# Third layer's attention loop: program order on four engines instead of one, and work dealt out by VectorE's time

## The chip, the core and the metric

The kernel runs on one core of a Trainium2 chip. A core has TensorE (PE in the profile; its weight loads are PEld), VectorE (DVE), ScalarE (ACT), GpSimd (POOL) and SyncE (SP), each with its own queue of instructions, which it takes in order; they meet through semaphores. The metric is the device time of one execution in microseconds, and the median of several runs counts. The kernel before took 3640.07 us (3 runs, 3638.57 to 3646.86).

## The reference

The program computes four blocks in a row on x of shape (8, 512, 128), all in float32. Each block takes a layer norm of x, runs a sequence mixer and a feed-forward net on it, and adds `s * silu(g)`. Only the last block, "layer 3", is touched by the change. Cut to what matters it is:

```python
xn = layernorm(x)
# mixer s: a state-space recurrence in chunks, 4 heads of 64, state 128
proj = xn @ W_in                       # z, x, B, C, dt, A, trap, angles
theta = cumsum(angles * dt)            # K, Q = rope(B, C + bias, theta)
S = (Q @ K.T) * decay * causal         # E in the kernel
y = S @ (c * x) + ein * (Q @ state) + coef * x
s = (y * silu(z)) @ W_out
# feed-forward g: 16 heads, softmax over the QUERIES of each key, no mask
scores = einsum('bqd,bkd->bkq', q, k) / sqrt(128)
out = einsum('bkq,bkv->bqv', softmax(scores), v)
g = l2norm(l2norm(out @ Wo) @ Wff); g = gelu(g)
x = x + s * silu(g)
```

The softmax is the large part: 8 batches x 16 heads x 512 x 512 scores.

## The kernel before

The block is built by `layer3` (L2025) with the class `Layer3`. The 16 heads of a batch are worked off in *units*: a unit is one group of four heads (`g`, 0 to 3) and one tile of 128 keys (`kc`, 0 to 3), so a batch has U = 16 units and the stage has 128. A unit has two halves:

- `scores` (L1960): four matmuls of 128 keys by 512 queries, each into a PSUM bank of its own ("pu"), each on a quarter of TensorE's rows (L1969). VectorE takes the negated maximum of each (`nm`, L1972), ScalarE the exponential with that bias, which also leaves the sum `sm` (L1973).
- `weigh` (L1940), LAG = 2 units later: VectorE inverts the sums (L1946), GpSimd scales the values (`va`, L1947), TensorE adds the products up over four key tiles in the bank "pf" (L1954), and every fourth unit the result `oT` is copied out.

Between the units other work of the block is fitted in. It is written as generators, which hand back control at every `yield`:

- `begin(b)` (L1705): layer norm of batch b, its transpose `xT`, queries, keys, values, and then `parameters` (L1744): the small quantities of the recurrence with a softplus polynomial on VectorE, the reciprocal root `r` on GpSimd (L1702), the angles and their sines.
- `mixer(b, jt)` (L1851): one chunk of 128 positions, four per batch. z and x from one matmul (L1857), kq on GpSimd (L1866), four rope products and two sums on VectorE (L1871 to L1873), decays E (L1878, L1883, masked on GpSimd at L199), two groups of transposes (L1897) copied to `kqT`, E times their product (L1902, L1903), the state (L1908 to L1914), the outputs y (L1920 to L1929), and y's transpose `yT` (L1935).
- `end(b)` (L1975): the output product with Wo, two norms with a product with Wff between, gelu, the product of the recurrence with W_out (L1994), and the store.

All these use PSUM banks of a third kind, "pa". Before, the eight banks are split 5 (pu), 1 (pf), 2 (pa).

Who runs when is set in two ways. TensorE's order is the program's: `manual_schedule(engines={PE})` at L2030. The orders of VectorE, ScalarE and GpSimd are chosen by the framework's scheduler, which simulates the program; scores and weigh get a high priority there (`AHEAD = 300`). The program itself gives the generators one step per unit: of those running, half go between scores and weigh and the rest after. A mixer starts at unit `at(b, jt)`, at the earliest one before its chunk's units, with the first ones spread by three units. `Kern.evac` (L115) copies a bank out with ScalarE and VectorE in turn.

Of the kernel before, what the change touches and what calls it, by code (L numbers as in the profile page):

```python
# [15 lines left out]
ALU = mybir.AluOpType  # L16
# [1598 lines left out]
def softplus(nc, pool, x):  # L1615

    shape = list(x.shape)
    tl = lambda name: pool.tile(shape, F32, name=name)
    e, z, q, p = tl("sp_e"), tl("sp_z"), tl("sp_q"), tl("sp_p")
    nc.scalar.activation(e, x, AF.Abs)  # L1620
    nc.scalar.activation(e, e, AF.Exp, scale=-1.0)
    yield
    nc.vector.tensor_scalar(z, e, 2.0, None, ALU.add)
    nc.vector.reciprocal(z, z)
    nc.vector.tensor_tensor(z, z, e, ALU.mult)
    nc.vector.tensor_tensor(q, z, z, ALU.mult)
    nc.vector.tensor_scalar(p, q, 1.0 / 17, None, ALU.mult)
    for n in range(15, 1, -2):
        nc.vector.scalar_tensor_tensor(p, p, 1.0 / n, q, ALU.add, ALU.mult)
    nc.vector.scalar_tensor_tensor(p, p, 1.0, z, ALU.add, ALU.mult)  # L1630
    nc.vector.tensor_scalar(x, x, 0.0, None, ALU.max)
    nc.vector.scalar_tensor_tensor(x, p, 2.0, x, ALU.mult, ALU.add)


class Layer3:
# [43 lines left out]
    def layernorm(self, x, xn):  # L1679

        k, nc = self.k, self.k.nc
        s1 = self.sp2.tile([P, JT], F32, name="s1")
        nc.vector.tensor_reduce(s1, x, AX.X, ALU.add)
        nc.vector.tensor_scalar(s1, s1, 1.0 / C, None, ALU.mult)
        nc.vector.tensor_tensor(xn, x, bc(s1, 2, C), ALU.subtract)
        r = self.rms(xn, JT, 1e-5)
        nc.vector.tensor_tensor(xn, xn, bc(r, 2, C), ALU.mult)

    def rms(self, x, n, eps, floor=False):


        nc = self.k.nc
        sq = self.tp.tile([P, n, C], F32, name="sq", bufs=1)
        nc.scalar.activation(sq, x, AF.Square)
        ss = self.sp2.tile([P, n], F32, name="ss")
# [5 lines left out]
        r = self.sp2.tile([P, n], F32, name="rs")  # L1701
        nc.gpsimd.tensor_tensor(r, ss, self.k.minus_half.to_broadcast([P, n]), ALU.pow)  # L1702
        return r

    def begin(self, b):  # L1705
# [3 lines left out]
        bt = slice(b * JT, (b + 1) * JT)  # L1709
        xn = tp.tile([P, JT, C], F32, name="xn3", bufs=1)  # L1710
        self.layernorm(self.x[:, bt, :], xn)
        yield
        xT = tp.tile([P, T + 1], F32, name="xT3")
        nc.gpsimd.memset(xT[:, T:], 0.0)
        k.to_features(xn, xT, nt=JT)
        yield
# [8 lines left out]
        nc.scalar.copy(q["kT"], ps)  # L1725
        ps = k.pa()
# [6 lines left out]
        yield  # L1733
# [3 lines left out]
        k.evac(q["V"], ps)  # L1737
        q["oT"] = tp.tile([P, 4, T], F32, name="oT3", bufs=1)
        q["held"], q["po"] = {}, {}
        yield  # L1740
        q["ready"] = True
        yield from self.parameters(q)

    def parameters(self, q):  # L1744
# [8 lines left out]
        for jt in range(JT):  # L1753
# [9 lines left out]
            if jt % 2:  # L1763
                yield
        r = self.rms(raw.rearrange("p j a n -> p (j a) n"), 2 * JT, 1e-5)
# [4 lines left out]
        nc.vector.tensor_scalar(beta[:, 0], beta[:, 0], 0.5, 0.5, ALU.mult, ALU.add)  # L1770
        nc.vector.tensor_scalar(beta[:, 1], beta[:, 1], -0.5, 0.5, ALU.mult, ALU.add)
# [5 lines left out]
        yield  # L1777
# [10 lines left out]
        yield  # L1788
        yield
# [6 lines left out]
        nc.vector.tensor_scalar(flat(v["ell"]), ps[:, 0, :], -1.0, None, ALU.mult)  # L1796
        nc.vector.tensor_tensor(v["eout"], v["eout"], v["c"], ALU.mult)
        yield
# [4 lines left out]
        for jt in range(JT):  # L1803
# [4 lines left out]
            if jt == 1:  # L1808
                yield
        yield  # L1810
# [3 lines left out]
        nc.vector.tensor_reduce(dot, prod, AX.X, ALU.add)  # L1814
        meet = par[:, :, NPAR + 4 :].rearrange("p j (a h) -> p j a h", a=2)
# [8 lines left out]
        yield  # L1824

# [12 lines left out]
        nc.vector.scalar_tensor_tensor(t, n, -TWO_PI[0], theta, ALU.mult, ALU.add)  # L1838
        for part in TWO_PI[1:]:
# [7 lines left out]
        nc.scalar.activation(n, n, AF.Square)  # L1847
        nc.vector.tensor_scalar(of(cos), n, -2.0, 1.0, ALU.mult, ALU.add)
        q.update(v=v, BC=BC, sin=sin, cos=cos, state=None)

    def mixer(self, b, jt):  # L1851
# [3 lines left out]
        tl = lambda name, *shape: mp.tile([P, *shape], F32, name=name)  # L1855
        ps = k.pa()
# [4 lines left out]
        nc.vector.scalar_tensor_tensor(z, z, 1.0, ps[:, 0:256], ALU.add, ALU.mult)  # L1861
        xv = tl("xv3", HM, HP)
        nc.scalar.copy(xv.rearrange("p h d -> p (h d)"), ps[:, 256:512])
        kq = tl("kq3", 2, HM, C)
        bias = cn["kq"].rearrange("p (a h n) -> p a h n", a=2, h=HM)
        nc.gpsimd.tensor_tensor(kq, bc(q["BC"][:, jt], 2, HM), bias, ALU.add)  # L1866
        sn, cs = (bc(q[n][:, jt], 1, 2) for n in ("sin", "cos"))
        x1, x2 = kq[:, :, :, 0:NA], kq[:, :, :, NA : 2 * NA]
        t = [tl(f"rope{i}", 2, HM, NA) for i in range(4)]
        for i, (a, r) in enumerate(((x1, cs), (x2, sn), (x1, sn), (x2, cs))):  # L1870
            nc.vector.tensor_tensor(t[i], a, r, ALU.mult)  # L1871
        nc.vector.tensor_tensor(x1, t[0], t[1], ALU.subtract)
        nc.vector.tensor_tensor(x2, t[2], t[3], ALU.add)  # L1873
        yield
# [6 lines left out]
        E = tl("E3", HM, P)  # L1881
# [3 lines left out]
        xc = tl("xc3", HM, HP)  # L1885
# [3 lines left out]
        if jt < JT - 1:  # L1889
            xe = tl("xe3", HM, HP)  # L1890
            nc.gpsimd.tensor_tensor(xe, xv, bc(v["eout"][:, jt, :], 2, HP), ALU.mult)
        yield
        kqT = tl("kqT3", 2, HM, C)
        for w in range(2):
# [3 lines left out]
            k.evac(kqT[:, w], ps)  # L1898
            yield
# [16 lines left out]
        yield  # L1916
        py = k.pa((P, 2, HM, HP))
        if state is not None:
            for h in range(HM):
                nc.tensor.matmul(py[:, 1, h, :], kqT[:, 1, h, :], state[:, h, :], start=True, stop=True)  # L1920
        for h in range(HM):
            nc.tensor.matmul(py[:, 0, h, :], E[:, h, :], xc[:, h, :], start=True, stop=True)
        nc.vector.tensor_tensor(y, y, py[:, 0], ALU.add)
        if state is not None:
            inter = tl("inter3", HM, HP)
# [4 lines left out]
        yield  # L1930
# [6 lines left out]
        q["mixed"] = jt  # L1937
        yield

    def weigh(self, b, u):  # L1940
# [3 lines left out]
        E, sm = q["held"].pop(u)  # L1944
        heads = lambda a: a.rearrange("p (i v d) -> p i v d", v=4, d=8)[:, :, g, :]
        nc.vector.reciprocal(sm, sm)  # L1946
        nc.gpsimd.tensor_tensor(heads(va[:, kc, 0:C]), heads(q["V"][:, kc, :]), bc(sm, 2, 8), ALU.mult)  # L1947
# [9 lines left out]
        if kc == JT - 1:  # L1957
            k.evac(q["oT"][:, g, :], q["po"].pop(g))

    def scores(self, b, u):  # L1960

        k, nc, q = self.k, self.k.nc, self.q[b]
        g, kc = divmod(u, JT)
        E, sm, nm = (self.ep.tile([P, 4, n] if n > 1 else [P, 4], F32, name=nm) for n, nm in ((T, "at3"), (1, "sm3"), (1, "nm3")))
        q["held"][u] = E, sm
        pus = [k.psum("pu", (P, T)) for _ in range(4)]
        for n, pu in enumerate(pus):
            r = slice(n * 32, n * 32 + 32)
            nc.tensor.matmul(pu, q["kT"][r, kc * P : (kc + 1) * P], q["qT"][r, g, :], start=True, stop=True)  # L1969
        for n, pu in enumerate(pus):  # L1970
            w = slice(n, n + 1)
            nc.vector.tensor_reduce(nm[:, w], pu, AX.X, ALU.max, negate=True)  # L1972
            nc.scalar.activation(E[:, n, :], pu, AF.Exp, bias=nm[:, w], accum_out=sm[:, w])  # L1973

    def end(self, b):  # L1975
# [11 lines left out]
        yield  # L1987
        while q.get("mixed") != JT - 1:
            yield
        s = tp.tile([P, JT, C], F32, name="s3", bufs=1)  # L1990
        ps = k.pa((P, JT, C))
        for jt in range(JT):
            for w in range(2):
                nc.tensor.matmul(  # L1994
                    ps[:, jt, :], q["yT"][:, w, jt, :], cn["W_out"][:, w * C : (w + 1) * C],
                    start=(w == 0), stop=(w == 1),
                )
        nc.scalar.copy(s, ps)
# [163 lines left out]
```

## Time and profile before

| quantity | value |
|---|---|
| median of 3 runs | 3640.07 us |
| the profiled execution's own time | 3631.03 us |
| its span | 3629.3 us |
| PE / DVE / ACT / POOL busy, whole span | 2764.3 / 2336.2 / 1642.4 / 745.4 us |
| layer 3: first constants loaded, to the end | 2628.4 to 3629 us |
| maxima L1972, mean of one | 683 ns |
| exponentials L1973, mean of one | 688 ns |
| mean granted TensorE clock, span / score loop | 0.835 / 0.86 of full speed |

A row of the groups reads: line, engine, operation, tile written <- tiles read, shapes, count | busy time in us, mean ns of one | idle time of the engine just before these instructions, and what ended most of it. A row of waits reads: who waited for whom: us in total, times, longest us. A row of the table of stretches has the busy time and the number of instructions of each engine, then the clock granted to TensorE, the DMA engines' busy share and their rate.

### The profile page before, as it was taken

Reading aid. Unit: us, or ns where it says so; the run is one execution under the profiler, and the core shown is the slowest. Engines: PE = TensorE matmul, PEld = TensorE weight load, DVE = VectorE, ACT = ScalarE, POOL = GpSimd, SP = SyncE. Lnnn points to the kernel's source line nnn. Section 1 sums busy time; section 2 is a strip of 40 time slices with the busy share of each in tenths; the row PEclk is TensorE's granted clock in tenths of the full one; section 3 lists DMA queues with packets and bytes.
Section 4 is the critical chain, followed back from the end, with each engine's and each line's share of the span. In section 5 each row is a group of like instructions: output and inputs, shape, how many; then the busy total and the mean of one; then the engine's idle time right before and its main releaser. Section 6 shows DMA issues by size and latency. Waiting matters only on the chain.

```text
span 3629.3 us, 44988 instructions
## 1 busy us (share of the span) xinstructions
PE 2764.3 (76%) x16390; PEld 1479.4 (41%) x16390; DVE 2336.2 (64%) x6346; ACT 1642.4 (45%) x3207; POOL 745.4 (21%) x845
## 2 busy tenths in 40 slices
PE   6164656512998898799999999998678877778777
PEld 4143444401444454344444444444334444444444
DVE  7989898998583234334445445445478787777776
ACT  5163545512544455233333333333266666655655
POOL 0004050400125553201101101101112222222121
PEclk8585757555789899799899899899878898878989
DMA  4003030311002222100000000000000000000000
GB/s 120 2 2 72 1 81 1 72 49 34 1 2 47 39 42 29 56 1 1 1 1 1 1 1 1 1 1 1 6 15 1 4 4 4 1 3 4 1 4 7
DMA packets 67519, 64.53 MB, mean 18 GB/s; under 512 B 5344, under 2 KB 59616, under 8 KB 66784
## 3 DMA queue, kind: packets, MB, share of 16 engines
q1 hardware_dynamic: 39264, 42.75, 3.8%
q0 software_dynamic: 19712, 14.69, 3.1%
q10 hardware_dynamic: 8320, 4.19, 0.4%
q8 instruction: 129, 2.11, 0.2%
q14 instruction: 94, 0.77, 0.1%
HBM read 43.80 MB, written 17.83 MB: 17 GB/s over the span
## 4 chain that ended last, share of the span: by engine, by line
PE 35%; DVE 16%; ACT 7%; issue 2%; POOL 2%; DMA 0%; POOLq 0%; ACTq 0%; DVEq 0%; SPq 0%
PE pa L1372 6%; PE pu L1390 6%; DVE nm L1972 4%; ACT at L1973 3%; PE pu L1969 3%; PE pf L1954 2%; DVE mpad L1404 2%; PE pf L1435 2%; PE pa L1486 1%; PE pa L1485 1%; ACT at L1422 1%; PE pa L1878 1%; PE pa L1509 1%; PE pa L1359 1%; PE pa L1515 1%
## 5 line engine op out<-in xcount | busy, mean ns | idle before, releaser
L1973 ACT ACTIVATE at<-pu,nm 128x512 f32<-128x512 f32 x512 | 347.9, 688 | 174.3 <-DVE nm L1972 154.5
L1972 DVE TENSOR_REDUCE nm<-pu 128x1 f32<-128x512 f32 x512 | 327.4, 683 | 75.4 <-PE pu L1969 74.8
L199 POOL TENSOR_SCALAR_AFFINE_SELECT at<-at 128x512 f32<-128x512 f32 x184 | 123.6, 672 | 1000.2 <-ACT at L1422 851.7
L1404 DVE TENSOR_REDUCE mpad<-pu 128x2 f32<-128x256 f32 (+3 forms) x256 | 199.2, 819 | 168.1 <-PE pu L1401 168.1
L1422 ACT ACTIVATE at<-pu 128x1024 f32<-128x1024 f32 (+3 forms) x256 | 171.8, 702 | 283.5 <-PE pu L1390 283.2
L1078 ACT ACTIVATE at<-pu,rsqrt 128x1024 f32<-128x1024 f32 (+3 forms) x256 | 191.1, 793 | 191.0 <-PE pu L1073 161.2
L1372 PE MATMUL pa<-hid,f 128*128 128x512 f32 x512 | 222.7, 593 | 0.0
L1969 PE MATMUL pu<-qT,kT 32*128 32x512 f32 x1024 | 203.1, 731 | 2.4 <-ACT at L1973 2.3
L1390 PE MATMUL pu<-qT,kT 32*128 32x512 f32 (+3 forms) x1024 | 160.6, 514 | 56.4 <-DVE mpad L1404 41.8
L748 PE MATMUL pa<-ident,Y 128*128 128x128 f32 x32 | 7.9, 425 | 211.2 <-DVE Y L739 211.2
L1954 PE MATMUL pf<-at,va 128*32 128x512 f32 x1024 | 163.1, 715 | 0.4 <-POOL va L1947 0.4
L1390 PE MATMUL pu<-kT,qT 32*128 32x128 f32 (+3 forms) x1024 | 150.8, 565 | 14.7 <-ACT at L1422 10.5
L548 POOL DMA_INDIRECT xg<-xn_d,idx x48 | 55.1, 1147 | 499.5 <-PE pf L552 318.5
L1372 PEld LDWEIGHTS pa<-hid,f 128*128 128x128 f32 x512 | 96.6, 190 | 119.5 <-issue 118.9
L1493 DVE SCALAR_TENSOR_TENSOR X<-X,u 128x512 f32<-128x512 f32 x56 | 38.7, 691 | 156.7 <-ACT u L1488 156.7
L1073 PE MATMUL pu<-qT,kT 32*128 32x512 f32 (+3 forms) x1024 | 130.3, 513 | 4.9 <-ACT at L1078 3.9
L1016 POOL DMA_INDIRECT f_d<-ys,idx x64 | 105.0, 1640 | 140.0 <-DMA f_d<-ys,idx 85.2
L1947 POOL TENSOR_TENSOR va<-V,sm 128x32 f32<-128x32 f32 x128 | 36.7, 286 | 463.6 <-DVE sm L1946 384.0
L1390 PEld LDWEIGHTS pu<-qT,kT 32*128 32x128 f32 x1024 | 67.3, 196 | 154.4 <-DVE mpad L1404 114.3
L1373 ACT ACTIVATE hid<-pa,f 128x512 f32<-128x512 f32 x64 | 44.0, 688 | 172.5 <-PE pa L1372 172.5
L1083 DVE TENSOR_TENSOR at<-at,ceiling 128x512 f32<-128x512 f32 x72 | 50.0, 695 | 102.3 <-ACT at L1078 91.4
L700 DVE TENSOR_TENSOR Z<-Hs,KE 128x96 f32<-128x96 f32 x510 | 108.8, 253 | 0.9
(610 smaller groups left out, 6682.8 us busy)
## 6 DMA issues: line engine op xcount, KB each, us to landing
w<-in_w_dram SPq DMA_DIRECT2D x24, 512.0 KB, 3.7
f_d<-zeros ACTq DMA_DIRECT2D x8, 512.0 KB
xn_d<-xn SPq DMA_DIRECT2D x8, 512.0 KB, 5.0
w<-in_w_dram SPq DMA_DIRECT2D x16, 256.0 KB, 3.2
w<-in_w_dram SPq DMA_DIRECT2D x24, 128.0 KB
f<-in_f_dram SPq DMA_DIRECT2D x1, 2888.0 KB, 11.9
xn<-in_x_dram SPq DMA_DIRECT2D x4, 512.0 KB, 9.0
Gt<-in_x_dram SPq DMA_DIRECT2D x4, 512.0 KB
```

What stands on the lines that cost most here:

```text
L199: self.nc.gpsimd.affine_select(a, a if src is None else src, pattern, ALU.is_ge, 0.0, base=0, channel_multiplier=-1)
L700: nc.vector.tensor_tensor(z[:, 0:3, v, :], bc(prev[:, v, :], 1, 3), bc(KE[:, o + t, 0:3, :], 2, 4), ALU.mult)
L1073: nc.tensor.matmul(pu[:, n, 0:m], q["kT"][r, g // 2, kc * P : kc * P + P], q["qT"][r, g, kc * P :], start=True, stop=True,)
L1078: nc.scalar.activation(at_[:, i : i + 2, 0:m], pu[:, :, 0:m], AF.Square, bias=k.rsqrt2, scale=32.0**-0.5)
L1372: nc.tensor.matmul(ps, fn[n][:, c0 : c0 + P], src[:, i, :], start=(i == 0), stop=(i == 3))
L1390: self.k.nc.tensor.matmul(pu[:, n, 0:m], a[r, c0 : c0 + P], b[r, q0 : q0 + m], start=True, stop=stop)
L1404: nc.vector.tensor_reduce(top[:, i : i + 2, 16], pu[:, :, 0:m], AX.X, ALU.max)
L1422: nc.scalar.activation(at_[:, i : i + 2, 0:m], pu[:, :, 0:m], AF.Exp, scale=8.0**-0.5)
L1954: nc.tensor.matmul(po[i * 32 : i * 32 + 32, :], va[:, kc, c0 : c0 + 32], E[:, i, :], start=(kc == 0), stop=(kc == JT - 1))
L1969: nc.tensor.matmul(pu, q["kT"][r, kc * P : (kc + 1) * P], q["qT"][r, g, :], start=True, stop=True)
L1972: nc.vector.tensor_reduce(nm[:, w], pu, AX.X, ALU.max, negate=True)
L1973: nc.scalar.activation(E[:, n, :], pu, AF.Exp, bias=nm[:, w], accum_out=sm[:, w])
```

## The change

Four things change in layer 3, and the arithmetic stays.

1. The program's order becomes the order of TensorE, VectorE, ScalarE and GpSimd.
2. Each generator's `yield` now gives an estimate of VectorE's time (us) in the step just done. A function `fill` is called twice per unit, between the second and third exponential and after weigh. It moves every mixer one step, and ends and the oldest begin only while a credit of 1.75 us per fill lasts. `yield 0.0` stands for a step without VectorE work; several stand alone between a step that makes something and the one whose products read it.
3. The PSUM banks are split 4 (pu), 1 (pf), 3 (pa). Copies that alternated between two engines get a fixed one, mostly ScalarE; the mixer's z and x are copied out of PSUM together (`zx`), and z's gate then reads that copy. Several mixer tiles have one buffer instead of two.
4. The reciprocal of the sums and the scaling of the values (`scale`) come out of weigh and run one unit after their scores. `rms` is parted into `squares` and `root`. W_out's product moves from `end` to the last mixer of a batch. In the outputs, E's products stand ahead of the state's. If a batch's parameters aren't finished when its first mixer is due, the rest of them is run out at once.

```diff
+    def squares(self, x, n, of):
+        sq = self.tp.tile([P, n, C], F32, name="sq" + of, bufs=1)
+        self.k.nc.scalar.activation(sq, x, AF.Square)
+        return sq
+    def root(self, sq, n, eps, of, floor=False):
...
+    def turned(self, src, dst, copy):
+        ps = k.pa((P, JT, P))
+        for i in range(JT):
+            k.nc.tensor.transpose(ps[:, i, :], src[:, i, :], k.ident)
+        copy(dst, ps.rearrange("p a b -> p (a b)"))
...
         nc.scalar.activation(z, ps[:, 0:256], AF.Tanh, scale=0.5)
-        nc.vector.scalar_tensor_tensor(z, z, 1.0, ps[:, 0:256], ALU.add, ALU.mult)
-        xv = tl("xv3", HM, HP)
-        nc.scalar.copy(xv.rearrange("p h d -> p (h d)"), ps[:, 256:512])
-        kq = tl("kq3", 2, HM, C)
+        zx = tl("zx3", 512)
+        nc.scalar.copy(zx, ps)
+        xv = zx[:, 256:].rearrange("p (h d) -> p h d", d=HP)
+        kq = one("kq3", 2, HM, C)
...
         nc.gpsimd.tensor_tensor(kq, bc(q["BC"][:, jt], 2, HM), bias, ALU.add)
+        yield 0.0
+        nc.vector.scalar_tensor_tensor(z, z, 1.0, zx[:, 0:256], ALU.add, ALU.mult)
...
         for i, (a, r) in enumerate(((x1, cs), (x2, sn), (x1, sn), (x2, cs))):
             nc.vector.tensor_tensor(t[i], a, r, ALU.mult)
+        yield 1.9
         nc.vector.tensor_tensor(x1, t[0], t[1], ALU.subtract)
         nc.vector.tensor_tensor(x2, t[2], t[3], ALU.add)
-        yield
+        yield 0.8
...
-            k.evac(kqT[:, w], ps)
-            yield
+            (nc.vector.tensor_copy if w else nc.scalar.copy)(kqT[:, w], ps)
+            yield 0.7 * w
+        yield 0.0
...
+    def scores(self, b, u):
...
+        for n, pu in enumerate(pus):
+            nc.vector.tensor_reduce(nm[:, n : n + 1], pu, AX.X, ALU.max, negate=True)
+        for n, pu in enumerate(pus):
+            w = slice(n, n + 1)
+            nc.scalar.activation(E[:, n, :], pu, AF.Exp, bias=nm[:, w], accum_out=sm[:, w])
+            if n == 1:
+                yield
+
+    def scale(self, b, u):
...
+        nc.vector.reciprocal(sm, sm)
+        nc.gpsimd.tensor_tensor(heads(va[:, kc, 0:C]), heads(q["V"][:, kc, :]), bc(sm, 2, 8), ALU.mult)
...
-            k.evac(q["oT"][:, g, :], q["po"].pop(g))
+            nc.scalar.copy(q["oT"][:, g, :], q["po"].pop(g))
...
-        ctx.enter_context(k.banks("l3p", pu=5, pf=1, pa=2))
+        ctx.enter_context(k.banks("l3p", pu=4, pf=1, pa=3))
         L = Layer3(k, ctx, x, A, at, k.out)
-        ctx.enter_context(k.tc.manual_schedule(engines={mybir.EngineType.PE}))
+        E = mybir.EngineType
+        ctx.enter_context(k.tc.manual_schedule(engines={E.PE, E.DVE, E.Activation, E.Pool}))
         U = 4 * JT
-        AHEAD = 300
+        SHARE = 1.75
-        EARLY, EVERY = 10, 3
-        at = lambda b, jt: max(b * U + jt * JT - 1, EARLY + EVERY * (b * JT + jt))
...
+        EARLY, EVERY = 9, 3
+        at = lambda b, jt: max(b * U + jt * JT - 2, EARLY + EVERY * (b * JT + jt))
...
+        def fill():
+            nonlocal credit
+            credit = min(credit, SHARE) + SHARE
+            for works in (mixers, ends, begins):
+                for w in works[:1] if works is begins else list(works):
+                    if works is mixers or credit > 0.0:
+                        cost = next(w, None)
+                        if cost is None:
+                            works.remove(w)
+                        else:
+                            credit -= cost
...
+                    if n == at(b, jt):
+                        for w in begins if "cos" not in L.q[b] else ():
+                            for _ in w:
+                                pass
+                            begins.remove(w)
+                            break
+                        mixers.append(L.mixer(b, jt))
...
+            scores = L.scores(*divmod(n, U)) if n < B * U else iter(())
+            next(scores, None)
+            fill()
+            next(scores, None)
             if LAG <= n < B * U + LAG:
-                with k.tc.high_priority(offset=AHEAD):
-                    L.weigh(*divmod(n - LAG, U))
-            step(len(todo))
+                L.weigh(*divmod(n - LAG, U))
+            if 1 <= n <= B * U:
+                L.scale(*divmod(n - 1, U))
+            fill()
```

## The prediction

> **What bounds the kernel now.** I read the table of stretches first, to size the stage. Only the third layer (numbered 3, the last) is edited; its score loop runs from 2646 to 3602 us.
>
> ```profile
> core 0: us, PE busy (x) PEld busy (x) DVE busy (x) ACT busy (x) POOL busy (x), PEclk, DMA share, GB/s
> 2628.00:2646.00 18.00, 8.59 (x31) 5.57 (x30) 10.83 (x24) 3.46 (x6) 3.56 (x6) 0.72 0.28 105
> 2646.00:3602.00 956.00, 757.09 (x4384) 404.90 (x4386) 727.08 (x1661) 589.00 (x1534) 214.34 (x314) 0.86 0.01 3
> 3602.00:3629.00 27.00, 12.17 (x94) 9.84 (x86) 8.24 (x16) 7.61 (x14) 2.27 (x3) 0.76 0.04 11
> ```
>
> In 956 us no engine is full: VectorE 727 (76%), TensorE 757 (79%), ScalarE 589 (62%). The loop has 128 units of four score tiles. The same table for the maxima's line alone gives the pace: 60 and 64 maxima per 128 us, so 16 units (a batch) take some 128 us, 8 us each, in the middle of the stage.
>
> ```profile
> 2832.00:2960.00 128.00, 38.57 (x60) 0.87 0.01 3
> 3088.00:3216.00 128.00, 40.38 (x64) 0.84 0.01 3
> ```
>
> The waits say who holds whom up: first VectorE's, then TensorE's list over this stretch.
>
> ```profile
> DVE nm L1972 <- PE pu L1969: 74.8, 69, 3.9
> DVE sm L1946 <- ACT at L1973: 47.0, 56, 1.6
> DVE z L1861 <- ACT z L1860: 37.0, 20, 4.4
> ```
>
> ```profile
> PE pa L1857 <- DVE E L1903: 28.8, 8, 5.6
> PE pa L1736 <- DVE E L1903: 19.6, 4, 4.9
> PE pa L1878 <- DVE E L1903: 17.7, 8, 4.2
> PE pa L1935 <- DVE y L1929: 12.8, 7, 3.4
> ```
>
> It is a ring: TensorE stands in its written order behind E or y, which VectorE was given late; the next scores then come late, and VectorE waits for them (74.8 us). Another 84 us it spends on a reciprocal or a gate put down before ScalarE has its input. So the stage is bound by order, and its floor is the fullest engine.
>
> **The floor of each engine after the change.** The costs, from the groups by shape and one unit's timeline:
>
> ```profile
> L1972 DVE TENSOR_REDUCE nm<-pu 128x1 f32<-128x512 f32 x512 | 327.4, 683 | 75.4 <-PE pu L1969 74.8
> L122 DVE COPY kqT<-pa 128x512 f32<-128x512 f32 x35 | 23.8, 681 | 3.8 <-PE pa L1897 3.8
> L120 ACT COPY kqT<-pa 128x512 f32<-128x512 f32 x29 | 17.3, 596 | 14.7 <-PE pa L1897 14.5
> L1863 ACT COPY xv<-pa 128x256 f32<-128x256 f32 x32 | 12.0, 374 | 10.1 <-DVE z L1861 10.0
> L2000 DVE TENSOR_TENSOR zo<-zo,rs 128x512 f32<-128x512 f32 x7 | 13.8, 1977 | 4.1 <-POOL rs L1702 4.1
> ```
>
> ```profile
> 2755.88 1.07 PE L1954 MATMUL pf<-at,va 128*32 128x512 f32 x8
> 2755.98 2.48 DVE L1972 TENSOR_REDUCE nm<-pu 128x1 f32<-128x512 f32 x4 [1.17 <-PE pu L1969]
> ...
> 2756.88 1.16 PE L1902 MATMUL pa<-kqT 128*128 128x128 f32 x8
> ```
>
> VectorE: the built orders show 28 fewer evacuations (15 of oT, 3 each of kqT, zT and xT, 4 of V), each 0.68 us: -19 us. Nothing else leaves or joins it: 727 - 19 = 708 us. ScalarE gets those 28 at 0.59 (+16.5), copies 512 columns instead of 256 in every mixer (32 x (0.59 - 0.37) = +7), and loses 4 table loads at 1.28 (-5): 607 us. GpSimd and the DMA queues issue what they did; the eight output DMAs keep their order.
>
> TensorE's instructions are the same, 757 us by the row. Here the Trainium skill ("Perfetto Trace Analysis", Identifying the Most-Contended Engine) says that matmul busy time does not measure headroom, and to take weight-load time, 405 us here. By the row TensorE would be the floor, 757; by the page it has room. I take neither, but the tightest groups of the trace: scores 1.14 and sums 1.07 per unit (x128 = 283); per mixer transposes 1.32, decays 1.16, z 1.12, products 1.16, outputs 1.06 + 1.10, state 1.00, y 0.44 (8.4, x32 = 267); about 21 per batch for projections and ends (x8 = 168). That is an estimate of 718 us, level with VectorE's 708. So the floor is about 710 to 720, if the order lets them overlap.
>
> **What the new order does to each wait.** The reciprocal moves to the following unit, between two fills, behind at least four more maxima: the 47 us go. z moves a half unit behind its tanh, with zx copied out: the 37 us go too, and the three pa banks are freed by copies on ScalarE. E, the state and y stand on VectorE in the half unit in which TensorE makes their products, never later, and TensorE uses them a unit on: of the waits on E and y nothing should be left.
>
> What is new is that VectorE cannot step past a product which isn't there. Queued behind it are the next four maxima, behind them the exponentials, behind those the next scores. Count from R, the first maximum of a unit. The maxima take 2.48; exponentials begin at R + 0.8 and end at R + 3.5 (4 x 0.67). With four banks the next unit's fourth score needs the last of them, so TensorE is free for other work at R + 3.5 + 1.1 = R + 4.6. If a unit lasts D, that is 4.6 - D after the next R, where VectorE reaches its first product at 2.48 + 0.18 = 2.7.
> - Output products (one unit in four): z 1.12, sums 1.07, outputs 2.1: ready at 8.9 - D, a stall of 6.2 - D.
> - Second transposes: 0.66, sums 1.07, 0.66: ready at 7.0 - D, a stall of 4.3 - D.
> - E: 1.07 + 1.16: ready at 6.8 - D, a stall of 4.1 - D.
>
> I added VectorE's instructions of one middle batch, unit by unit in the built order, at their rows' means: between 3.8 and 11.4, mostly 5 to 7 us. Against these D only two of twelve products stall, 1.4 and 0.5: some 2 us per batch. Two more places: the parameters' last part is run out in one go ahead of the next batch's first mixer, and its cosine waits for ScalarE's two sines and a square (0.63 + 0.61 + 0.62, and a table load of 1.28 if that isn't early): about 3 us with the maxima standing behind. The gelu sits between the second and third exponential, with a load each way (2 x 1.28 + 1.26): it holds exponentials back 3.8 us, which I put at 3 on the path. The fills' other products (Wo alone is 3.7 on TensorE) push scores now and then: between 0 and 8, I take 6, since the two floors are so close. Sum 14 us per batch; over seven (first and last have less of each), 98 us.
>
> z now reads zx from SBUF. The skill ("SBUF — State Buffer", SBUF: two separate sides) speaks against that: a VectorE operation with two SBUF inputs and a GpSimd operation that reads SBUF exclude each other for the whole instruction. The trace agrees for zo above, 1977 ns in the mean against 693 at the least. Read so, each z could wait out kq, a 2.0 us GpSimd row: 32 x 2.0 = 64 us. I take 0: the four rope products behind z wait for that same kq anyway. If kq is late, z only waits in their place.
>
> Ahead of the loop 2 us of parameter matmuls (2644.6 to 2646.6) move behind the first scores, and the ending chain (27 us) keeps its steps; I count both at nothing.
>
> **The sum.** Loop: 708 + 98 = 806 us instead of 956, a gain of 150. The profiled execution took 3631 (span 3629.3): 3481. The median of the runs is 9 above it: 3490. VectorE would be at 88% of the loop.
>
> **The rivals.**
> 1. *The gain stops halfway.* The four banks close a loop over ScalarE: whatever a fill puts between exponentials 2 and 3 (z and zx 1.0, kqT 0.6, tables) delays two scores of the next unit, and the two nearly level floors don't interleave. At 7.0 us a unit the loop takes 896 and the kernel 3580. For it: ScalarE goes to 607 us, and it would need only 1.3 us of stall per unit over 708/128 = 5.5. Against: the D above absorb up to 2 us.
> 2. *Almost no stalls*, 30 us in all: loop 738, kernel 3422. Against: TensorE's estimated 718 beside it.
> 3. *Slower.* Each product of E, kqT and y is met too early in every unit, since ordered VectorE has no other work to put there, where the planner had. It decides from (956 - 708)/128 = 1.9 us of stall per unit. At 2.3 us the loop takes 1002, the kernel 3686. For it: the waits of 3.4 to 5.6 us in TensorE's list, turned round. Against: without any cover D falls to 4.2, 3.6 and 3.3 ahead of the three products, and the stalls come to 2.0 + 0.7 + 0.8 = 3.5 us per four units, where 7.6 are needed.
>
> That the change doesn't take hold is excluded by the built orders: maxima now stand four together throughout, with one reciprocal half a unit later.
>
> **How the numbers follow.** First case 0.60 (own range 3450 to 3550: 58 to 158 us of stall), rival 1 0.20, rival 2 0.08, rival 3 0.12. About 0.2%, 7 us, is what these runs can tell from no change; only the seam of rivals 1 and 3 lies there, 0.02. Faster 0.87, slower 0.11. The range runs to rival 2 below and past the centre of rival 1 above: 3425 to 3600.
>
> **What would show it.** Loop near 806 us, VectorE near 708 of it, over 85%; maxima of a middle batch (64) in about 108 us; no sm or z wait of note on VectorE; TensorE's waits on E and y gone and replaced by short waits on exponentials; VectorE's remaining waits on TensorE at kqT, y and the maxima, under 100 us. Wrong if those waits sum to over 240, if the maxima wait for scores as now, or if the granted clock falls below 0.86: at 0.70, seen in one 50 us stretch, TensorE's 718 would be 882.

## The result, and the profile after

The changed kernel took 3621.46 us (median of 5 runs, 3617.50 to 3629.25); the kernel before, run beside it, 3638.57 (3636.30 to 3646.86). The ratio is 0.9952, with a 95% interval of 0.9937 to 0.9968: 17 us faster, where 150 were forecast, and above the range of 3425 to 3600. The profiled execution lies 8 us above that median (3629.25, span 3627.5), the one of before 8 below its own (3631.03, span 3629.3), so the two traces show how the waits moved, and of the 17 us only 2.

The table of stretches of the changed kernel, over the score loop:

```profile
core 0: us, PE busy (x) PEld busy (x) DVE busy (x) ACT busy (x) POOL busy (x), PEclk, DMA share, GB/s
2646.00:3602.00 956.00, 824.75 (x4424) 437.96 (x4422) 721.85 (x1649) 592.67 (x1563) 202.13 (x315) 0.84 0.01 3
```

The loop still fills the same 956 us, and VectorE is at 76% of it as before (721.85 against 727.08). TensorE is busy 68 us longer (757.09 before), with the same matmuls. Of VectorE's waits in this stretch these matter:

```profile
DVE nm L1988 <- PE pu L1986: 93.2, 49, 6.8
DVE par L1777 <- ACT raw L1776: 30.5, 18, 3.4
DVE E L1925 <- PE pa L1924: 26.7, 19, 4.3
DVE kqT L1919 <- PE pa L1918: 15.0, 10, 3.3
DVE cos L1864 <- ACT turns L1862: 14.9, 8, 1.9
DVE y L1946 <- PE pa L1945: 6.1, 3, 2.5
DVE z L1886 <- ACT zx L1880: 5.3, 8, 2.1
```

The waits that the change was to take away are nearly gone: `sm` fell from 47.0 to 1.1, `z` from 37.0 to 5.3. Others stand in their place, and the sum over all of VectorE's rows is what it was: 224.7 us before, 225.5 after. TensorE's list was turned over as well. Its matmuls no longer wait for E or y (a weight load still does, 3.8 us for y in all); it waits for exponentials (first its matmuls, then its weight loads; the two overlap in time and are not to be added):

```profile
PE pu L1986 <- ACT at L1991: 86.8, 33, 8.9
PEld pu L1986 <- ACT at L1991: 161.1, 151, 9.1
```

The groups by shape show the same from the side of the work, first the scores before, then the changed kernel:

```profile
L1969 PE MATMUL pu<-qT,kT 32*128 32x512 f32 x1024 | 203.1, 731 | 2.4 <-ACT at L1973 2.3
...
L1991 ACT ACTIVATE at<-pu,nm 128x512 f32<-128x512 f32 x512 | 348.0, 690 | 197.3 <-DVE nm L1988 193.8 <-POOL E L199 1.5 <-POOL xc L1907 1.3
L1988 DVE TENSOR_REDUCE nm<-pu 128x1 f32<-128x512 f32 x512 | 318.6, 680 | 93.3 <-PE pu L1986 93.2
L1986 PE MATMUL pu<-qT,kT 32*128 32x512 f32 x1024 | 284.8, 735 | 87.3 <-ACT at L1991 86.8
...
L1886 DVE SCALAR_TENSOR_TENSOR z<-z,zx 128x256 f32<-128x256 f32 x32 | 26.3, 822 | 5.3 <-ACT zx L1880 5.3
```

Read the first three rows of the changed kernel as a circle: exponentials wait for maxima, maxima for scores, scores for exponentials. And look at the scores' busy time. It was 203.1 us before, with 2.4 us of idle time ahead of it and a mean of 731 ns for one; now it is 284.8 with a mean of 735. The single matmul is no slower. A unit's four scores sit on four row groups, and released together they overlap: the timeline shows units of 1.14 us. Now each bank is let go by an exponential of its own, so they often start one after another; a unit's scores keep TensorE busy for 2.2 us in the mean (284.8 / 128), where it was 1.6 (203.1 / 128). One such place, TensorE's timeline:

```profile
3198.80 2.74 PE L1986 MATMUL pu<-qT,kT 32*128 32x512 f32 x4 [3.28 <-ACT at L1991]
3201.47 1.94 PE L2016 MATMUL pf<-at,va 128*32 128x512 f32 x8
...
3203.81 1.92 PE L1899 MATMUL pa<-upto,adt 128*128 128x128 f32 x8
```

After 3.28 us of waiting, the last two scores take 2.74 us, and then the sums and decays, 1.06 each at their tightest, take 1.94 and 1.92. The clock granted in the same place (the third value from the right):

```profile
3195.00:3198.80 3.80, 0.52 (x5) 0.01 (x1) 2.05 (x8) 3.73 (x8) 0.24 (x1) 1.00 0.00 0
3198.80:3201.50 2.70, 2.70 (x8) 0.82 (x10) 2.70 (x8) 1.20 (x3) 0.00 (x0) 0.55 0.00 0
3201.50:3206.00 4.50, 4.50 (x21) 2.74 (x21) 3.85 (x8) 2.81 (x10) 0.24 (x1) 0.51 0.02 4
3206.00:3210.00 4.00, 4.00 (x31) 1.99 (x30) 2.42 (x5) 2.59 (x10) 2.36 (x4) 1.00 0.23 66
```

For 7 us behind the gap TensorE has half of its clock: here it has waited itself slow. (The Trainium skill, "TensorE: Matmul & The Clock Gate", HAM oscillation, puts such a loss of clock behind idle gaps of more than about 3.4 us; the one here is 3.28 in the matmuls and 4.11 in the weight loads.)

By batches, counted from 1 and from first maximum to first maximum: batches 4 to 7 of the eight took 125.7 us each in the mean before and now take 119.4, 119.5, 119.5 and 119.5, where the forecast had 108. Batch 3 takes 147.9 (125.2 before); two of its units take 23.3 and 21.6 us, in which parameters are run out at once. So in the two traces batch 3 alone gives back 23 of the 25 us that batches 4 to 7 gain.

### The profile page after: what moved, and what is told of

The parts are those of the page before. It is cut to its first block, busy times and chain, and to the rows that moved or that the text cites. A ratio compares the mean times of both kernels' runs of the same rounds, so it can differ in the third digit from the quotient of the medians.

```text
span 3627.5 us, 45015 instructions
## 1 busy us (share of the span) xinstructions
PE 2834.9 (78%) x16390; PEld 1512.1 (42%) x16390; DVE 2323.2 (64%) x6318; ACT 1643.5 (45%) x3231; POOL 733.2 (20%) x845
## 4 chain that ended last, share of the span: by engine, by line
PE 41%; DVE 15%; ACT 7%; POOL 2%; issue 2%; DMA 1%; POOLq 0%; ACTq 0%; another core or an unknown queue 0%; DVEq 0%; SPq 0%
PE pa L1372 6%; PE pu L1390 6%; PE pu L1986 5%; PE pf L2016 2%; DVE nm L1988 2%; DVE mpad L1404 2%; ACT at L1991 2%; PE pf L1435 2%; PE pa L1486 1%; PE pa L1485 1%; ACT at L1422 1%; PE pu L1073 1%; PE pa L1509 1%; PE pa L1007 1%; PE pa L1359 1%
## 5 line engine op out<-in xcount | busy, mean ns | idle before, releaser
L1988 DVE TENSOR_REDUCE nm<-pu 128x1 f32<-128x512 f32 x512 | 318.6, 680 | 93.3 <-PE pu L1986 93.2
L1986 PE MATMUL pu<-qT,kT 32*128 32x512 f32 x1024 | 284.8, 735 | 87.3 <-ACT at L1991 86.8
L1986 PEld LDWEIGHTS pu<-qT,kT 32*128 32x128 f32 x1024 | 94.6, 213 | 176.7 <-ACT at L1991 161.1
L1390 PE MATMUL pu<-kT,qT 32*128 32x128 f32 (+3 forms) x1024 | 153.2, 575 | 14.9 <-ACT at L1422 10.7
L1372 PEld LDWEIGHTS pa<-hid,f 128*128 128x128 f32 x512 | 96.6, 190 | 119.5 <-issue 118.9
L1390 PEld LDWEIGHTS pu<-qT,kT 32*128 32x128 f32 x1024 | 67.8, 199 | 155.3 <-DVE mpad L1404 114.8
```

Source lines behind the costliest of these rows:

```text
L1372: nc.tensor.matmul(ps, fn[n][:, c0 : c0 + P], src[:, i, :], start=(i == 0), stop=(i == 3))
L1390: self.k.nc.tensor.matmul(pu[:, n, 0:m], a[r, c0 : c0 + P], b[r, q0 : q0 + m], start=True, stop=stop)
L1988: nc.vector.tensor_reduce(nm[:, n : n + 1], pu, AX.X, ALU.max, negate=True)
```

## The experiments

Each ratio is to the kernel before, run beside it. Where two runs are compared, the difference is that of their ratios, times 3638 us, if nothing else is said.

### Whose order costs

The first theory was that VectorE in program order stands in line behind products. The list of engines in program order was cut down in three ways, and the kernel before was put into its own program order on all four.

```diff
-        ctx.enter_context(k.tc.manual_schedule(engines={E.PE, E.DVE, E.Activation, E.Pool}))
+        ctx.enter_context(k.tc.manual_schedule(engines={E.PE}))                     # only TensorE
+        ctx.enter_context(k.tc.manual_schedule(engines={E.PE, E.DVE}))              # TensorE and VectorE
+        ctx.enter_context(k.tc.manual_schedule(engines={E.PE, E.Activation, E.Pool}))  # all but VectorE
```

Only TensorE:

> The changed program with only TensorE in program order; the scheduler orders VectorE, ScalarE and GpSimd again, without the priority that the kernel before gave to the scores. Theory A (TensorE standing in its scores with four banks eats the gain of the order): the order still gives something, so this is slower than the changed kernel's 3621 us, about 3660. Theory B (units of unlike size under a fixed order eat it): a scheduler can even them out, so this is as fast or faster, 3560 to 3620.

Measured: 3595.12, ratio 0.9877 (0.9839 to 0.9914), 27 us under the changed kernel. The scheduler's orders of this program are better than the program's own.

TensorE and VectorE:

> The changed kernel with program order on TensorE and VectorE alone; ScalarE and GpSimd are ordered by the scheduler. If VectorE's order is what costs against the scheduler's (0.988): as the changed kernel, 0.995. If it is ScalarE's (exponentials behind copies, par behind gelu): as with the scheduler, 0.988.

Measured: 3627.49, 0.9982 (0.9973 to 0.9992), 11 us slower than the changed kernel.

All but VectorE:

> TensorE, ScalarE and GpSimd in program order, VectorE alone ordered by the scheduler. With only TensorE in program order the time was 3595 (0.988 of before), with all four 3621. If VectorE's fixed order is what costs (theory 2): 3590 to 3605. If ScalarE's and GpSimd's cost it: 3615 to 3630.

Measured: 3617.53, 0.9940 (0.9922 to 0.9958). So neither VectorE's order alone nor that of ScalarE and GpSimd alone costs the 27 us: to free VectorE gains 4 us, which the intervals don't tell from nothing, to free the other two loses 11, and only both together gain. That one fixed order is enough to hold the others in step is a reading of this, not shown.

Only TensorE, with scores, weigh and scale at the high priority that they had before:

> The changed program with only TensorE in program order, and scores, sums and scaling in the scheduler's high priority as in the kernel before. If the priority was what evened out the kernel before: better than without it, 0.980 to 0.986. If it only puts VectorE's maxima ahead of what TensorE stands and waits for, as before: 0.990 to 1.000.

Measured: 3606.59, 0.9932 (0.9913 to 0.9951). VectorE's wait for the sums is 76.3 us (57.5 without the priority), and nothing is gained: by the ratios it is 20 us slower than without.

The kernel before, with all four engines in its program order:

```diff
-        ctx.enter_context(k.tc.manual_schedule(engines={mybir.EngineType.PE}))
+        ctx.enter_context(k.tc.manual_schedule(engines={E.PE, E.DVE, E.Activation, E.Pool}))
```

> The kernel before with its program order on all four engines, nothing else changed: its steps have no empty places between a product and its reader. If the order alone is what helps, 3600 to 3630. If the order needs the empty steps and the reciprocal a unit later, which is what I expect, the products are met too early and it is slower than the 3639 of before: 3680 to 3800.

Measured: 4195.22, 1.1540 (1.1494 to 1.1586). The order alone costs 557 us, far more than was expected. The rest of the change (empty steps, moved operations, banks, fixed copies) wins that back, and 17 us more; which part of it does was not taken apart.

### Whose work bounds

Half of the sums of weigh left out (TensorE's work, some 68 us at 1.07 per unit):

```diff
-        for i in range(4):
+        for i in range(4) if kc in (0, JT - 1) else ():
```

> The changed kernel without the products of scores and values for the second and third key tile of each group, so half of these sums is left out: 64 x 1.07 = 68 us less of TensorE, nothing else. If TensorE sets the pace throughout: -68 us, 3553. If VectorE does: 3621. Theory B (each unit lasts as long as its fuller engine): about half, 3585. Theory A (TensorE idles in the scores, so the time isn't its own work): 3600 to 3621.

Measured: 3623.10, 0.9961 (0.9951 to 0.9971): nothing gained. The stretch and one group of this run:

```profile
2646.00:3602.00 956.00, 813.16 (x3936) 470.15 (x3936) 716.99 (x1645) 591.91 (x1563) 202.36 (x316) 0.80 0.01 3
```

With some 480 matmuls fewer TensorE is busy nearly as long, at a granted clock of 0.80 instead of 0.84. Scores went from 285 to 323 us (735 to 792 ns for one) and the products in the third kind of bank from 467 to 490. So 68 us less of TensorE's work gain nothing. Whether its work is no bound, or the lower clock gave the time back, this run alone does not tell.

The maxima taken over half of the columns (VectorE, 134 us of work less, 318.6 to 184.5; the maximum is then that of half the scores):

```diff
-            nc.vector.tensor_reduce(nm[:, n : n + 1], pu, AX.X, ALU.max, negate=True)
+            nc.vector.tensor_reduce(nm[:, n : n + 1], pu[:, 0 : T // 2], AX.X, ALU.max, negate=True)
```

> The changed kernel with each maximum taken over the first 256 of 512 columns, the other half of the columns left out of it: 512 x about 0.27 = 138 us less of VectorE, and the first exponential of a unit starts 0.27 us sooner, the last 1.1 us. If VectorE sets the pace throughout: -138 us, 3483. If TensorE's own work does: 3621. Theory B: about half, 3550. Theory A: the ring from maximum to exponential to next score gets 1.1 us shorter in units where TensorE stands, also some 3520 to 3560; the two theories part in the run with half the sums.

Measured: 3569.28, 0.9808 (0.9771 to 0.9844): 52 us of 134. Of what VectorE is spared on the very link of the circle, more than half is lost again in waits (the maxima's for scores rises from 93 to 110). The edit shortens the circle too, so it does not say how much of the 52 us is VectorE's work as such.

Gelu and the sines replaced by tanh, so that ScalarE loads one table where it loaded 32 (31 loads of 1.28 us less, 40 us in all):

```diff
-        nc.scalar.activation(f, f, AF.Gelu)
+        nc.scalar.activation(f, f, AF.Tanh)
-        nc.scalar.activation(of(sin), t, AF.Sin)
-        nc.scalar.activation(n, t, AF.Sin, scale=0.5)
+        nc.scalar.activation(of(sin), t, AF.Tanh)
+        nc.scalar.activation(n, t, AF.Tanh, scale=0.5)
```

> The changed kernel with tanh in place of the third layer's gelu and sines, so another function is computed there and ScalarE never changes its table in this layer. Each batch loses up to four loads of 1.28 us, 8 x 5.1 = 41 us of ScalarE. Theory C (ScalarE's tables between the exponentials stall the scores; the prediction put 3 us per batch on the path for gelu and part of 3 for the cosine): 20 to 40 us less, 0.984 to 0.990 of before. Theory D (all engines are coupled in one ring, so a wait that is taken away comes back elsewhere): under 10 us, 0.993 to 0.996.

Measured: 3578.84, 0.9854 (0.9835 to 0.9872), some 36 us faster (27 to 44 by the two intervals). ScalarE is 62% busy, and yet most of these 40 us are on the path: a load stands between two exponentials, and the circle runs through them.

The product with Wo, 3.79 us in one piece in the trace, dealt out over several fills (one empty step after each of its four groups):

```diff
+            yield 0.0
```

> The changed kernel with the product with Wo (3.7 us on TensorE in one step) dealt out over five fills, a quarter in each of the first four. Theory B (TensorE's lumps, which the credit in VectorE's time does not count, make VectorE wait 4.25 us for scores there in each batch): 15 to 30 us less, 0.987 to 0.991 of before. Theory D: 0.993 to 0.997.

Measured: 3612.48, 0.9943 (0.9926 to 0.9961), not to be told from the changed kernel's 0.9952. The maxima's wait fell from 93 to 62.5, and the time did not follow.

### Loosening the order

Two scores, other work, two scores:

```diff
-        for n, pu in enumerate(pus):
+        for two in ((0, 1), (2, 3)):
+            for n in two:
...
+            if two == (0, 1):
+                yield
```

> The changed kernel with a unit's four scores parted: two scores with their maxima and exponentials, the first fill, then the other two. Theory A (TensorE stands in the scores, 158 us of waits on exponentials up to 3570 us, while products of the fill stand behind them): it now has the fill's products to do while the third and fourth exponential of the unit before run, so the waits fall below 100 us and the kernel to 3540 to 3590. Theory B (unlike units): no change to speak of, 3610 to 3630. Against both: VectorE meets the fill's products sooner, which alone would make it slower, 3640 to 3700.

Measured: 3695.27, 1.0181 (1.0157 to 1.0206), 83 us slower than the changed kernel.

The first fill after the fourth exponential instead of the second:

```diff
-            if n == 1:
+            if n == 3:
```

> The changed kernel with the first fill behind the fourth exponential instead of between the second and the third. Theory C (what ScalarE does between the exponentials, z and zx 1.0, kqT 0.6, gelu with two table loads 3.8 us, holds back two scores of the next unit): some 12 us per batch come off the scores' wait, 3560 to 3600. Otherwise 3610 to 3630.

Measured: 3639.38, 1.0021 (1.0011 to 1.0030), 25 us slower. The maxima's wait falls to 70, that of the parameters rises to 43. Worked out over the 128 units of its trace, the fourth exponential ends 3.64 us behind its unit's first maximum in the mean (4.67 in the changed kernel), and batches 4 to 7 still take 119.5 us each. So ScalarE's other work between the exponentials is not by itself what holds them.

The credit per fill 2.25 instead of 1.75:

```diff
-        SHARE = 1.75
+        SHARE = 2.25
```

> The changed kernel with 2.25 instead of 1.75 us of credit per fill, so that the parameters of a batch are through, or nearly, when its first mixer is due, and no long stretch of VectorE work is run out at once. Theory B (units of 18.8, 23.3 and 21.6 us in batches 1 and 2, 13.2 us in each later one): these units shrink, and 30 to 60 us come off, 3560 to 3590. If the work has only moved to other units that were full too: 3610 to 3630.

Measured: 3634.87, 1.0012 (1.0000 to 1.0025), 22 us slower. The longest units shrink from 23.3 to 18.4 us, batch 3 stays at 147.2, and batches 5 to 7 grow to 122.9. The maxima's wait is 72.5, but that of y 35.7 instead of 6.1.

Five score banks and two others:

```diff
-        ctx.enter_context(k.banks("l3p", pu=4, pf=1, pa=3))
+        ctx.enter_context(k.banks("l3p", pu=5, pf=1, pa=2))
```

> The changed kernel with the banks of before, five for scores and two for the rest. If the lost fifth score bank is what makes TensorE wait (one score of the next unit could go ahead without an exponential): 3590 to 3610. If the third bank for the rest is worth more, because copies run a half unit later: slower, 3640 to 3700.

Measured: 3636.95, 1.0016 (1.0003 to 1.0028), 23 us slower. Weight loads wait 87.5 us for exponentials instead of 161, the maxima 114.7 instead of 93. In all four runs one wait shrank and another grew. None of these runs isolates the circle itself, since none gives it a second unit of banks.

### Opening the circle

The banks are used up (4, 1 and 3 of eight), so the circle can only be opened with smaller scores. In the next kernels scores are made for 256 of the 512 queries, two heads to a bank from the same row group; maxima and exponentials read those columns twice, so that VectorE and ScalarE do what they did, and a tight unit on TensorE takes 1.14 us as before. The other half of the queries is left out, and two of four heads repeat the scores of their neighbours. A unit then takes two banks: with four, two units fit (ring2), with two, one (ring1).

```diff
-        pus = [k.psum("pu", (P, T)) for _ in range(4)]
+        pairs = [k.psum("pu", (P, 2, T // 2)) for _ in range(2)]
+        pus = [pair[:, i, :] for pair in pairs for i in range(2)]
...
-            r = slice(n * 32, n * 32 + 32)
+            r = slice(n // 2 * 64, n // 2 * 64 + 32)
...
-        ctx.enter_context(k.banks("l3p", pu=4, pf=1, pa=3))
+        ctx.enter_context(k.banks("l3p", pu=2, pf=1, pa=3))   # ring1 alone
```

> The same half of the scores in two banks only, so that the banks hold one unit as in the changed kernel. Both theories: within 25 us of the changed kernel's 3621, since the work of each engine and the depth of the ring are what they are there; the maxima's wait for scores at 75 to 115 us.

Measured: 3678.00, 1.0104 (1.0087 to 1.0121). Its waits are the changed kernel's, somewhat larger; it was expected within 25 us of 3621 and came 55 above. One difference shows in the traces: a unit's first exponential starts 1.39 us behind its first maximum (median of 128 units), in the changed kernel 0.78. So this circle is some 0.6 us longer, and ring1 is no equal of the changed kernel. Why is not shown. Ring2 has the same 1.39, so these two can be compared.

> Scores are made for 256 of the 512 queries, two heads to a bank, each head pair from one row group (so TensorE's time for a unit stays about what it was), and maxima and exponentials read the 256 columns twice, so that VectorE and ScalarE do as much as before; the result for the other half of the queries, and for two of four heads, is left out. A unit of scores takes two banks, the four banks hold two units. If the ring of one unit holds the loop (theory): the exponentials of the unit before are no longer waited for, TensorE's waits of scores for exponentials fall from 248 us (87 of a matmul's, 161 of a weight load's) under 80, the maxima's wait for scores from 93 us under 40, and the run is 50 us or more faster than ring1: 3560 or less. If the fixed order and the products behind it hold it (rival): the waits move to the parameters, the products and the exponentials, and the run is within 15 us of ring1.

Measured: 3591.71, 0.9865 (0.9848 to 0.9882): 86 us faster than ring1, with the same work, and 32 us faster than the changed kernel. TensorE's and VectorE's leading waits in ring1:

```profile
PEld pu L1989 <- ACT at L1994: 157.7, 70, 8.9
PE pu L1989 <- ACT at L1994: 127.2, 62, 8.7
DVE nm L1991 <- PE pu L1989: 105.0, 65, 6.0
```

and in ring2:

```profile
PEld pf L2021 <- POOL va L2008: 97.5, 53, 7.1
DVE nm L1991 <- PE pu L1989: 71.2, 27, 6.6
PE pf L2021 <- POOL va L2008: 65.5, 42, 6.7
```

Scores no longer wait for exponentials (4.4 us of idle time ahead of them, 129.6 in ring1), and their busy time goes from 257.7 us to 173.2. The granted clock of the loop is 0.82, against 0.79 in ring1, which may be a part of the gain. But the maxima still wait 71 us, expected were under 40, and the time missed the expected 3560: in program order TensorE now stands before the sums, for GpSimd's scaled values.

Is that the next bound? Each unit weighed one unit later, with one more buffer of exponentials:

```diff
+LAG3 = 3
...
-        self.ep = self.pool("e", LAG + 2)
+        self.ep = self.pool("e", LAG3 + 2)
...
```

> The kernel with two units of half scores in four banks (3592), with each unit weighed three units after its scores and not two (one more buffer for the exponentials). The same parts of the result are left out as there. If TensorE's waits for GpSimd's scaled values (163 us of the loop) are what took the place of the ring: they fall under 30, and the time to 3535 to 3570. If they only stood in time that VectorE's work needs anyhow: within 12 us of 3592.

Measured: 3615.53, 0.9925 (0.9904 to 0.9945), 22 us slower than ring2. (The 163 us expected away are the two rows above added up, though they overlap.) TensorE's waits for the scaled values are gone (7.5 us are left); TensorE waits for the copies of oT (75.4 us) and the exponentials for maxima 212 instead of 193. So the waits for scaled values had stood in time that was lost anyhow. What is left with the circle open is the order:

> The kernel with two units of half scores in four banks, and only TensorE in the order of the program. If the ring and the fixed order of the other three engines cost in different places, their gains add: 30 less than 3592 or more, 3540 to 3565. If the scheduler's order had its gain from working round the ring: 3580 to 3600.

Measured: 3494.76, 0.9605 (0.9579 to 0.9632). With two units of banks and only TensorE in program order the time comes near the 3490 forecast, but in a kernel that makes half of the scores. Its leading waits on ScalarE and VectorE:

```profile
ACT at L1994 <- DVE nm L1991: 57.7, 49, 4.1
DVE nm L1991 <- PE pu L1989: 34.0, 35, 2.9
```

The exponentials' wait for maxima was 194 in the changed kernel. The two causes do more together than apart: against the changed kernel free orders alone gained 27 us, the open ring alone 32, and both 126. How much the ring alone costs under free orders has no control here (ring1 was not run so).

At last the whole computation, nothing left out: two scores, other work, two scores, as in the split that cost 83 us, but with only TensorE in program order.

> The whole computation: two scores, other work, two scores, with only TensorE in the order of the program. With all four engines in program order this split cost (3695 against 3621), since every two maxima then had a place of their own in VectorE's order. If the scheduler makes use of the looser ring, two banks free while the other two are read: 3530 to 3585, under the 3595 of the unsplit one. If the split only doubles the number of times that scores wait for exponentials: 3600 to 3660.

Measured: 3562.78, 0.9812 (0.9796 to 0.9828). It beats the kernel before by 68 us and the changed one by 51, and the unsplit one with free orders by 24. The same split is a loss under four fixed orders and a gain under one. Why it gains is not shown: weight loads of scores wait as long for exponentials as in the unsplit kernel (79 and 81 us), so that two banks are refilled while the other two are read remains the expectation's reading.

## Why the prediction was wrong

The direction was right, the size was not: 17 us of 150. Step by step:

- *What bounds the kernel, "the stage is bound by order"*: right, and it went on being so. With half of the sums the time stayed (0.9961, at a lower clock), and half of the maxima's columns gained 52 of 134 us.
- *The floors.* VectorE: 708 forecast, 722 measured in the stretch. The step "I take 0" for z reading zx from SBUF was wrong by 13 us: nine of z's 32 instances ran beside a `kq` of GpSimd and took 1.69 to 2.05 us, each ending 0.28 us behind it; the other 23 took 0.42. This agrees with the rule of the Trainium skill ("SBUF — State Buffer", SBUF: two separate sides), which had announced up to 64 us; the collisions all lie in the first three batches. The rest of the 14 is a sum of rows that moved both ways: 8 us came in from ahead of the loop and behind it, the rope products fell by 5 (56.6 to 51.2), zo fell from 13.8 to 5.0, the gelu's input f rose from 6.8 to 12.7. ScalarE: 607 forecast, 593 measured. TensorE's 718: its records show 825, but the scores make 82 us more of that than before, since they were let go one by one. Where the banks and the orders were free, TensorE's records showed 704, VectorE's 702, and the kernel took 3495. So no run contradicts the floors. The Trainium skill's reading ("Perfetto Trace Analysis", Identifying the Most-Contended Engine) that matmul busy time is no good measure of headroom holds here: it rose by 68 us while no work was added.
- *The removed waits*: right. sm (47) fell to 1.1 and z (37) to 5.3 on VectorE, and TensorE's matmuls wait for E and y no more.
- ***The step that failed* is the sum of new stalls, "14 us per batch; over seven, 98 us".** VectorE's rows of waits come to 225.5 us, where these 98 were all that was to be left. Term by term over the loop: maxima waiting for scores, put at 42 (6 a batch, "between 0 and 8"), measured 93.2; products E, kqT and y, put at 14 (2 a batch, "only two of twelve products stall"), measured 26.7 + 15.0 + 6.1 = 47.8; the parameters' copy behind gelu and its loads, put at 21, 30.5 at `par` alone; the cosine, put at 21, 14.9; the copies of queries (qT), counted at nothing, 14.5. The rest are small rows.
- *Why it failed.* The working began at "exponentials begin at R + 0.8 and end at R + 3.5", took TensorE to be free at R + 4.6, and set against it a unit's length D from VectorE's sum. Worked out over the 128 units of the trace, the fourth exponential ends at R + 4.24 in the median (4.67 in the mean), since 131 us in all pass between second and third exponentials (6 before), and the next scores are through at R + 6.97 (mean 7.16), at R + 4.73 at the earliest. So the circle of banks was counted at its shortest. The count also takes the units as even, and they are not: from 3229 to 3263 us VectorE is busy 90% and TensorE 78%, from 3263 to 3320 it is TensorE 88% and VectorE 66%. In the latter a product of 3.79 us stands between two units' scores:

```profile
3277.86 3.79 PE L2029 MATMUL pa<-f,oT 128*128 128x128 f32 x32
...
3282.74 1.89 DVE L1988 TENSOR_REDUCE nm<-pu 128x1 f32<-128x512 f32 x3 [4.25 <-PE pu L1986]
```

  With one unit of banks VectorE has nothing in store to bridge it. That lump itself is not the cause, though: dealt out, it changed nothing; nor is the late fourth exponential by itself, which the run with the fill behind it mended without gain. Shown to recover the forecast time is only both together, two units of banks and free orders, and that in the kernel with half of the scores. How the loss divides between them in the whole computation stays open.
- *Rival 1* ("four banks close a loop over ScalarE") had this part of the mechanism at 0.20, with 60 of the 150 us left. Its counter-argument, "the D above absorb up to 2 us", is what the traces refute: the longest wait of a score for an exponential is 9.1 us. Shown for it: ring2, 86 us against ring1 and 32 against the changed kernel, and the table loads, 36 of 40 us. Its size was too small; the fixed orders add to it, which no case had: "ordered VectorE" stood under rival 3 as a thing of single products.
- *Shown-wrong signs*: two of the three came: the maxima wait for scores as before (93.2 against 74.8), and the clock fell to 0.84. VectorE's waits on TensorE came to 141 us (93.2 + 26.7 + 15.0 + 6.1), over the 100 forecast, not over the 240 named.

## What to carry to other kernels

Before counting on the floor of the fullest engine, follow the ring of buffers between engines once around. Where it holds one unit, a removed wait can come back at the next link, as here, and an engine in it can cost time though it is idle for more than a third of the time (here ScalarE with its table loads). A program order on several engines at once lost against the scheduler's here, with one unit of banks (27 us) and with two (95 us). So try the order on one engine first, and try a finer release of buffers again after freeing the orders, since the same edit can change its sign. Don't judge an engine by its busy time alone: take work away from it, and read the granted clock beside the time. Here TensorE gave up 68 us of work and stayed nearly as busy, at a lower clock.

## What was not expected of the hardware

- Matmuls on four row groups overlap as far as they start together: a unit's scores took 1.14 us at the tightest and 1.6 in the mean before, and 2.2 in the mean when four exponentials released the banks one by one, with each matmul as long as before (735 and 731 ns). The Trainium skill ("TensorE: Matmul & The Clock Gate", Part 3) tells of the overlap; the price of a spread start is this trace's.
- TensorE's clock went down with its work: with half of the sums left out the granted clock of the loop went from 0.84 to 0.80 and the time stayed (3623 and 3621). Behind one gap of 3.28 us it went from 1.00 to 0.55. In the kernel before in four program orders, with TensorE waiting most, it was 0.70.
- A gate whose two inputs lie in SBUF took 1.69 to 2.05 us instead of 0.42 where it met GpSimd's `kq`, nine times of 32; the mean doubled.
